# A four-layer graph network: the order of instructions planned with small GpSimd operations as users of the port shared with VectorE

## Chip, cores, metric

One core of one Trainium2 chip runs the whole kernel. The metric is device time in microseconds of one execution; the kernel before took 2909.99 us (median of 3 runs, 2907.28 to 2910.49).

## What is computed

32 graphs (batches) of 512 nodes with 128 features each, and a 0/1 adjacency matrix per graph with some 16 neighbours per node. Four layers, each on relu(layernorm(x)) and added to x:

```python
# layer 0: max over neighbours of relu(p_i + q_j + b)
p = h @ (W1 - W2); q = h @ W2
x = x + max_j(relu(p[:, :, None] + q[:, None, :] + b) * adj[..., None])
# layer 1: four steps, earlier features concatenated in the last two
src_agg = l2norm(adj, 2) @ (f @ ws + bs); dst_agg = l2norm(adj, 1).T @ (f @ wd + bd)
f = tanh(concat(src_agg, f @ wn + bn, dst_agg) @ wu + bu)
# layer 2: row-normalised aggregation
x = x + (adj / rowsum) @ (h @ weight) + bias
# layer 3: four GRU steps
m = adj.T @ (h @ weight[i]); h = gru_cell(m, h)
```

## The kernel before, in words

**Work.** Function `batch` makes the instructions of one graph: `prepare` (normalisation, transposed adjacency `at`, the table of q rows in DRAM, neighbour counts `cc` and `ccd`, keys of the remaining neighbours), `gathers` (layer 0), `layer1` and `layer23`. Features are held as 128 x (4 x 128) tiles, one PSUM bank each. Aggregations (`pg`) run as pairs of fp32r matmuls, one with `hi`, the value rounded to fp32r, and one with `lo`, the rest: ACT writes `hi`, VectorE (for `xn` GpSimd) writes `lo = source - hi`, and the matmuls follow (`parts`, L956, and `sbuf_parts`).

Layer 0's maximum comes from two sources. For each of four blocks of 128 columns and each of four slots, a one-hot matrix `oh` (VectorE compares `ccd` with a number, 128 x 1024) picks rows of q by matmul (`pa`), and VectorE takes the maximum into `acc`: 32 of these a batch. What is left, up to seven neighbours a node, comes by indirect DMA from the table on GpSimd's queue into `G`, 28 a batch, and VectorE takes the maximum into `gm` (L1127), 24 a batch.

A normalisation (`norm`) is done four times a batch: statistics on VectorE, then on GpSimd `rstd` as a power (a tensor_tensor on 128 x 4, L924) and `shift` as a product (128 x 4, L927), then `xn` on ACT. Before layer 1, GpSimd also works out the degrees' scales on 128 x 8 and 128 x 4 tiles (`dm`, `vectors`, `g`, `dinv`). In each GRU step, VectorE makes `nn`, ACT the tanh, GpSimd `zc = 1 - z` and the wide product `gate = h * z` (128 x 512, L1331), VectorE `nn * zc` and `h`; then `ph` transposes, and `hi` and `lo` follow for the next step.

**Order.** No order is written out by hand. Class `Flow` collects the operations, each with a planned cost, and works out when each engine issues what, in the manner of a list scheduler; the program's instruction order on each engine is the order in which `step` (L481) takes them. On the chip, the engines follow these queues and wait for each other's semaphores.

- `start` (L466) tells when an operation could begin: inputs ready, engine free, buffer free, and, for one with `port` set, not before `self.port`, the planned end of the last operation that uses the port (L477, L512). So no two marked operations overlap in the plan.
- Of those that can begin first, `step` takes the one with the earliest due time. `close` (L436) sets it: the place of the batch times `PACE`, less the length of the work behind it, less a lead. `LEADS` holds the lead of each stage, `LEADS0` and `LEADSN` what is added for the first and the last batch.
- `FIRST` and `LAST` shift the places of the first and last batches (L1365), and `WEIGHTS` gives the places of the three parts that load and fold the weights (`first`, `rest`, `last`). Up to six parts are open at once (`AHEAD`), so batches interleave. `SPACING` keeps the maxima of the gathered rows apart. `FIRST`'s fourth and `LAST`'s fifth value: the former is used from batch 3 on, the latter is not used with 32 batches.
- Buffers come in rings and are given out in the order in which the parts asked for them: `w3` of part `last` uses the buffer `nn` (L816), after the four `bfull` of part `rest` (L801).
- Where the plan has a gap of over 1 us on TensorE, it fills in matmuls without use (`spin`).

Every operation is noted by `Engine.note`, which marks the port's users (L295 to L298): on VectorE and on GpSimd's operations whose names begin with `tensor`, those with two inputs in SBUF of 64 or more elements per partition, and VectorE's tensor_scalar in any case. Issued instructions carry line L529 in the profile, where the plan calls them; they are told apart by their tiles.

## Time and profile before

| | |
|---|---|
| median of 3 runs | 2909.99 us |
| profiled execution, its own time | 2910.69 us |
| its span in the profile | 2909.0 us |
| granted TensorE clock, mean | 0.993 |
| busy: PE, DVE, ACT, POOL | 2795.8, 2299.1, 1268.4, 1848.5 us |
| wide GpSimd products `gate`, 128 x 512 | 124, mean 1365 ns |
| GpSimd `rstd` power, 128 x 4 | 128, mean 1193 ns |
| GpSimd `shift` product, 128 x 4 | 128, mean 287 ns |
| VectorE `gm` maximum, 128 x 128 | 768, mean 322 ns |
| VectorE `oh` compare, 128 x 1024 | 492, mean 723 ns |

PE stands for TensorE's matmuls, PEld for its weight loads, DVE for VectorE, ACT for ScalarE, POOL for GpSimd. A line of a group or a timeline names the tile that is written, then those that are read. A wait `A <- B: total, times, longest` is idle time of A's engine that B ended. The span of 2909.0 us leaves 1.7 us of the execution's time around it.

### The profile page before, as it was taken

To read this page: it belongs to the slowest core of one execution; us is meant where nothing else is said; L and a number is where in the kernel's file an instruction comes from. 1 tells how busy PE (TensorE), PEld (TensorE's weight loads), DVE (VectorE), ACT (ScalarE), POOL (GpSimd) and SP (SyncE) were. 2 spreads that over 40 slices of the span, in tenths; PEclk is the share of its full clock that TensorE was granted. 3 is DMA by queue.
4 is the path that set the end of the run, shared out by engine and by line. 5 is a ranking of instruction groups with operands and counts; after the bars stand their busy time and mean duration, and the time that the engine had idled before them with its cause. 6 is when DMAs were issued, how large, how long until landed. Compare 5 with 4: busy or idle time off the path is not lost.

```text
span 2909.0 us, 38588 instructions
## 1 busy us (share of the span) xinstructions
PE 2795.8 (96%) x11766; PEld 1794.6 (62%) x11766; DVE 2299.1 (79%) x5371; ACT 1268.4 (44%) x2622; POOL 1848.5 (64%) x2020
## 2 busy tenths in 40 slices
PE   7799999999999999999999999999999999999998
PEld 4565566666666665666665666666666666566675
DVE  6778888788888888888788888888888888887634
ACT  6643344444444443444443444444444444443333
POOL 3666656666666766666766666776666666666522
PEclk9999999999999999999999999999999999999999
DMA  6644334323444433334423344433344433333200
GB/s 150 136 74 88 62 85 81 83 55 76 79 86 81 83 60 78 74 83 80 87 56 78 74 84 87 82 69 64 74 84 87 81 81 56 70 66 63 55 5 9
DMA packets 191270, 218.49 MB, mean 75 GB/s; under 512 B 30376, under 2 KB 139600, under 8 KB 191056
## 3 DMA queue, kind: packets, MB, share of 16 engines
q0 software_dynamic: 47104, 92.34, 23.1%
q1 hardware_dynamic: 73768, 63.63, 7.1%
q10 hardware_dynamic: 70184, 59.98, 6.8%
q8 instruction: 96, 1.57, 0.2%
q14 instruction: 118, 0.97, 0.1%
HBM read 164.32 MB, written 17.96 MB: 63 GB/s over the span
## 4 chain that ended last, share of the span: by engine, by line
PE 85%; DVE 7%; DMA 2%; issue 2%; ACT 2%; POOL 1%; SPq 0%; ACTq 0%; DVEq 0%; POOLq 0%
PE pg L529 26%; PE pu L529 19%; PE pk L529 14%; PE pa L529 7%; PE phn L529 4%; PE pxn L529 4%; DVE acc L529 3%; PE ph L529 2%; PE pq L529 2%; PE pkey L529 2%; PE pt L529 1%; DVE lo L529 1%; PE pf L529 1%; PE po L529 1%; PE px L529 1%
## 5 line engine op out<-in xcount | busy, mean ns | idle before, releaser
L529 POOL DMA_INDIRECT G<-qtab,idx x768 | 841.3, 1095 | 653.6 <-DVE gm L529 495.3
L529 DVE TENSOR_TENSOR acc<-acc,pa 128x512 f32<-128x512 f32 x992 | 673.4, 679 | 123.3 <-PE pa L529 97.6
L529 PE MATMUL pg<-an,lo 128*128 128x512 f32 (+1 forms) x1072 | 461.9, 433 | 0.0
L529 PE MATMUL pg<-an,hi 128*128 128x512 f32 (+1 forms) x1072 | 456.1, 428 | 4.8 <-PE spin L553 1.1
L529 PE MATMUL pa<-oh,qhl 128*128 128x512 f32 x1024 | 450.5, 508 | 6.1 <-DVE acc L529 2.1
L529 PE MATMUL pu<-ag,w 128*128 128x512 f32 (+1 forms) x952 | 448.0, 568 | 4.1 <-DVE ag L529 4.1
L529 DVE TENSOR_SCALAR oh<-ccd 128x1024 fp32r<-128x1024 bf16 x492 | 348.9, 723 | 62.4 <-PE pa L529 55.0
L529 ACT ACTIVATE xn<-x,shift,rstd 128x128 f32<-128x128 f32 x512 | 214.6, 483 | 261.4 <-POOL shift L529 255.7
L529 PE MATMUL pg<-at,lo 128*128 128x512 f32 (+1 forms) x672 | 295.9, 442 | 22.8 <-DVE lo L529 22.3
L529 PE MATMUL pg<-at,hi 128*128 128x512 f32 (+1 forms) x672 | 272.7, 407 | 8.4 <-ACT hi L529 7.2
L529 PEld LDWEIGHTS pa<-oh,qhl 128*128 128x128 f32 x1024 | 191.8, 193 | 135.5 <-issue 65.9
L529 PEld LDWEIGHTS pg<-an,hi 128*128 128x128 f32 x1072 | 202.6, 189 | 107.2 <-issue 62.5
L529 PEld LDWEIGHTS pg<-an,lo 128*128 128x128 f32 x1072 | 202.7, 189 | 85.9 <-issue 52.0
L529 PE MATMUL pk<-h,g_hh 128*128 128x512 f32 (+1 forms) x528 | 246.7, 582 | 1.2 <-DVE ag L529 1.1
L529 DVE TENSOR_TENSOR gm<-gm,G 128x128 f32<-128x128 f32 x768 | 242.4, 322 | 3.5 <-DMA G<-qtab,idx 3.3
L529 PE MATMUL pk<-mT,g_ih 128*128 128x512 f32 (+1 forms) x528 | 243.3, 580 | 0.5 <-ACT mT L529 0.5
L529 PEld LDWEIGHTS pu<-ag,w 128*128 128x128 f32 x952 | 177.0, 189 | 107.7 <-issue 80.3
L529 ACT ACTIVATE gate<-pk,bsum 128x512 f32<-128x512 f32 (+1 forms) x264 | 176.7, 672 | 151.3 <-PE pk L529 148.7
L529 DVE TENSOR_TENSOR ag<-pg,rbc 128x512 f32<-128x512 f32 (+1 forms) x272 | 172.5, 653 | 71.5 <-PE pg L529 69.7
L529 DVE SCALAR_TENSOR_TENSOR nn<-phn,bcol,gate 128x512 f32<-128x512 f32 (+1 forms) x132 | 96.3, 729 | 148.2 <-ACT gate L529 148.1
L529 ACT COPY mT<-pg 128x512 f32<-128x512 f32 (+1 forms) x164 | 94.3, 575 | 272.9 <-PE pg L529 265.4
L529 POOL TENSOR_TENSOR rstd<-rstd,mhalf 128x4 f32<-128x4 f32 x128 | 152.7, 1193 | 86.9 <-DVE shift L529 82.6
(178 smaller groups left out, 5146.7 us busy)
## 6 DMA issues: line engine op xcount, KB each, us to landing
af<-in_adj_dram ACTq DMA_DIRECT2D x32, 1024.0 KB
ccd<-cc SPq DMA_DIRECT2D x512, 64.0 KB
an<-in_adj_dram POOLq DMA_DIRECT2D x128, 256.0 KB, 3.4
x<-in_x_dram ACTq DMA_DIRECT2D x64, 256.0 KB
rbc<-scal SPq DMA_DIRECT2D x32, 512.0 KB
G<-qtab,idx POOLq DMA_INDIRECT x768, 3.9
qtab<-qn SPq DMA_DIRECT2D x128, 64.0 KB
out_dram<-xo ACTq DMA_DIRECT2D x32, 256.0 KB
```

The source lines that it names most:

```text
L529: op.fn(*(real(v) for v in op.args), **{k: real(v) for k, v in op.kw.items()})
```

## The change

The mark of the port's users is widened: on GpSimd, an operation whose name begins with `tensor` and that has more than one input in SBUF is now marked, whatever its size. That adds the power and the product of each normalisation, and of the scales the power, `g`, `dinv` and the difference into `vectors`; those with one tensor input (`dm`, `has`, the copies) stay unmarked. The planner's numbers are replaced: `PACE`, `SPACING`, all leads but one, `FIRST`, `LAST`, `WEIGHTS`. What is computed, the tiles, the buffers and the planner's costs stay.

```diff
--- before.py
+++ after.py
@@ -33,39 +33,39 @@
 CODES = ((0, 1), (P, 1), (2 * P, 2), (4 * P, 4))
 ONACT = (2, 2, 1, 0)
 NLEFT = 7
-PACE = 46.14
-SPACING = 1.5
+PACE = 46.21
+SPACING = 1.6
 AHEAD = 6
 BANKS = (1, 2, 2, 1)
 
 LEADS = {
-    "prepare": -28.3, "counts": -7.5, "keys": 16.5, "rows": 26.6,
-    "gather0": 59.4, "gather1": 70.0, "gather2": 28.0, "gather3": 53.5,
-    "first": 61.2, "layer1": 43.0, "layer10": 30.3, "layer11": 8.7,
-    "layer12": 56.0, "layer13": -41.3, "layer2": 39.7, "layer3": 5.5,
-    "layer30": 99.5, "layer31": 189.8, "layer32": 213.5, "layer33": 84.7,
-    "out": 56.0,
+    "prepare": -28.3, "counts": 31.4, "keys": 20.4, "rows": 36.3,
+    "gather0": 70.0, "gather1": 75.0, "gather2": 44.1, "gather3": 65.1,
+    "first": 71.0, "layer1": 67.5, "layer10": 34.6, "layer11": 10.8,
+    "layer12": 54.1, "layer13": -65.5, "layer2": 38.2, "layer3": -10.5,
+    "layer30": 194.3, "layer31": 203.4, "layer32": 212.8, "layer33": 61.6,
+    "out": 87.1,
 }
 
 LEADS0 = {
-    "prepare": 18.5, "counts": 53.1, "keys": 4.8, "rows": -15.7,
-    "gather0": 52.2, "gather1": 93.4, "gather2": -34.5, "gather3": -69.1,
-    "first": 0.5, "layer1": 141.7, "layer10": 10.1, "layer11": 110.3,
-    "layer12": -73.8, "layer13": -13.4, "layer2": 6.9, "layer3": 56.5,
-    "layer30": 35.3, "layer31": 29.8, "layer32": 117.9, "layer33": 64.0,
-    "out": 75.9,
+    "prepare": 16.8, "counts": 45.5, "keys": -53.7, "rows": 3.2,
+    "gather0": 48.0, "gather1": 111.6, "gather2": 10.0, "gather3": 31.0,
+    "first": 77.1, "layer1": 209.2, "layer10": 0.7, "layer11": 111.5,
+    "layer12": -121.4, "layer13": -40.0, "layer2": -47.4, "layer3": 77.7,
+    "layer30": -5.6, "layer31": 99.0, "layer32": 161.7, "layer33": 176.6,
+    "out": 115.8,
 }
 LEADSN = {
-    "prepare": -19.9, "counts": -18.3, "keys": -42.0, "rows": 46.6,
-    "gather0": 15.9, "gather1": -47.7, "gather2": -77.8, "gather3": -4.3,
-    "first": 13.3, "layer1": -33.7, "layer10": 14.0, "layer11": -36.5,
-    "layer12": 103.7, "layer13": 62.6, "layer2": 212.2, "layer3": 99.8,
-    "layer30": 182.6, "layer31": 105.8, "layer32": 85.0, "layer33": 161.6,
-    "out": -15.2,
+    "prepare": 54.1, "counts": 28.9, "keys": -55.6, "rows": 8.4,
+    "gather0": 36.6, "gather1": -111.0, "gather2": -41.4, "gather3": -58.4,
+    "first": 0.8, "layer1": 3.9, "layer10": 6.0, "layer11": 6.3,
+    "layer12": 124.9, "layer13": 106.3, "layer2": 260.5, "layer3": 98.5,
+    "layer30": 146.5, "layer31": -13.0, "layer32": 15.9, "layer33": 155.6,
+    "out": -150.5,
 }
-FIRST = (1.57, 0.36, -0.05, 0.0)
-LAST = (0.0, 0.18, 0.33, 0.24, 0.3)
-WEIGHTS = (-3.98, -2.44, -5.94)
+FIRST = (1.4, 0.75, 0.18, 0.0)
+LAST = (0.0, -0.73, -1.07, -1.18, -4.34)
+WEIGHTS = (-4.28, -2.74, -9.33)
 
 LATE = {
     "xn2": ("xn0", 1), "hi2": ("qn", 1), "lo2": ("gm", 1), "mT": ("acc", 1), "hg": ("hT0", 1),
@@ -295,7 +295,8 @@
             tensors = [v for v in ins if v.free_size() >= 64 and in_sbuf(v)]
             fast = self.name == "vec" and op == "tensor_scalar"
             if self.name == "vec" or (self.name == "pool" and op.startswith("tensor")):
-                self.flow.part[-1].port = fast or len(tensors) > 1
+                two = self.name == "pool" and sum(in_sbuf(v) for v in ins) > 1
+                self.flow.part[-1].port = fast or two or len(tensors) > 1
 
         return note
 
```

## The prediction

> **What bounds the kernel now.** I read five views in this order: busy times on the page, windows of one batch length, TensorE's waits, the timelines around its idle stretches, and what VectorE's port users cost beside each kind of GpSimd work.

> The page, engines first:

> ```profile
> PE 2795.8 (96%) x11766; PEld 1794.6 (62%) x11766; DVE 2299.1 (79%) x5371; ACT 1268.4 (44%) x2622; POOL 1848.5 (64%) x2020
> PE   7799999999999999999999999999999999999998
> ```

> TensorE is busy all along but for the start and the end. Windows of 86.4 us (columns: stretch, its length, then busy us and count of PE, PEld, DVE, ACT, POOL, granted clock, DMA share, GB/s) show a loop that repeats exactly:

> ```profile
> 20.00:106.40 86.40, 60.06 (x334) 39.61 (x335) 61.09 (x149) 62.18 (x136) 44.28 (x58) 0.90 0.71 148
> 106.40:192.80 86.40, 75.58 (x420) 57.76 (x419) 70.17 (x189) 49.56 (x99) 61.53 (x67) 0.96 0.51 100
> ...
> 797.60:884.00 86.40, 84.77 (x352) 53.97 (x352) 71.47 (x167) 37.70 (x78) 57.86 (x63) 1.00 0.39 77
> 884.00:970.40 86.40, 84.77 (x352) 53.95 (x352) 71.42 (x167) 37.69 (x78) 58.07 (x63) 1.00 0.38 77
> ```

> One batch takes 86.4 us, TensorE is busy 84.77 of it and VectorE 71.4. Matmul ends are modelled, so I also summed starts: where they are dense, the start of the next comes 228 ns after a 128x512 fp32r matmul, 429 after a pass of an fp32 one, 109 after a 128x128 transpose. By these, a batch has 82.0 us of matmul work, 0.65 us of filling matmuls (spin) and 3.7 us of idle time. So an order can win at most 4.4 us a batch, and it can lose any amount. The waits say at what:

> ```profile
> PE pg L529 <- DVE lo L529: 22.3, 25, 1.1
> PE spin L553 <- DVE lo L529: 9.4, 25, 0.7
> ```

> 25 times each: two places in each batch of the loop. Here is the first, in the timelines of TensorE, VectorE and GpSimd (start, us, engine, work):

> ```profile
> 987.43 0.50 PE L529 MATMUL pg<-at,hi 128*128 128x512 f32 x1 [0.23 <-ACT hi L529]
> 987.91 0.51 PE L529 MATMUL pg<-an,hi 128*128 128x512 f32 x1
> 989.31 0.50 PE L529 MATMUL pg<-at,lo 128*128 128x512 f32 x1 [0.89 <-DVE lo L529]
> ```
> ```profile
> 985.95 1.31 DVE L529 TENSOR_TENSOR gm<-gm,G 128x128 f32<-128x128 f32 x1
> 987.18 1.47 DVE L529 TENSOR_TENSOR acc<-acc,pa 128x512 f32<-128x512 f32 x2
> 988.57 0.68 DVE L529 TENSOR_TENSOR lo<-pf,hi 128x512 fp32r<-128x512 f32 x1
> ```
> ```profile
> 985.80 1.31 POOL L529 TENSOR_TENSOR gate<-h,gate 128x512 f32<-128x512 f32 x1
> ```

> The gm maximum takes 1.31 us instead of its median of 0.28, because GpSimd's wide product began just before it. That pushes two acc maxima and then lo by 1.03 us, and the aggregation waits for lo. This place costs 1.9 us a batch by matmul starts. The second (ph, then hi, then lo, then the aggregation with an) costs 1.5 us, spin included, and has no such collision in it.

> [...] I sorted the trace's port users of VectorE by what they overlap most: gm beside a wide GpSimd instruction takes 1175 ns (34 of them), beside an rstd power 281 (36), beside nothing 280. oh takes 997, 692 (30) and 683. One such pair:

> ```profile
> 528.48 0.69 DVE L529 TENSOR_SCALAR oh<-ccd 128x1024 fp32r<-128x1024 bf16 x1 [0.69 <-PE pa L529]
> ```
> ```profile
> 528.04 1.17 POOL L529 TENSOR_TENSOR rstd<-rstd,mhalf 128x4 f32<-128x4 f32 x1
> ```

> The oh lies inside the power's 1.17 us and loses nothing. [...]

> **The change, part by part.** (1) *The mark.* It adds 12 GpSimd instructions a batch to the planner's port users: 4 rstd powers (mean 1193 ns), 4 shift products (287), the power and the difference into vectors (1681, 219), g (216) and dinv (208): 4.77 + 1.15 + 1.68 + 0.22 + 0.22 + 0.21 = 8.25 us. The wide ones were marked already. Nothing is added to the program: no instruction, wait or DMA; only the order on each queue changes. If the mark kept every small one clear of VectorE, VectorE would win 0.4 us in the whole run (all of its lengthening of over 60 ns beside small ones), and GpSimd some 19 us (128 x (1193 - 1044, the fastest tenth)) + 12 us (128 x (287 - 193)), about 1 us a batch on an engine at 64%. Behind GpSimd's shift stands ACT's xn, for which TensorE waits 8.6 us in all, nearly all before the loop. Value taken: 0; bounds 0 to -8.

> (2) *What the false exclusion does to the order.* VectorE's port users are about 55 a batch (24 gm, 15 oh, 4 nn products, 4 h, junk, qhl and small scalars). In the plan each now meets a small GpSimd instruction with a chance of 8.25 / 86.4 = 9.5%, and is put back by about half of 1.1 us: 55 x 0.095 x 0.5 = 2.6 us a batch of delay that the chip doesn't have. The planner answers by putting something else first. Where oh or gm moves, acc work hides it (TensorE waits 2.1 us for oh in the whole run). Where nn or h is put behind an acc or oh (0.7 us each), the next GRU step starts later, and what is late is hi, then lo: the waits above. I take a fifth (nn and h are 8 of 55, with something for lo being displaced): 0.5 us x 25 = +13. Bounds: 0, as the planner may fill with other batches' work, to +28 (one full 1.1 us displacement a batch at one of the two places). A gain is not excluded either: any new order draws the collisions anew, rival one below.

> (3) *Leads, pace, spacing.* PACE moves by 0.15%, nothing. SPACING 1.5 to 1.6 stretches the 24 spaced gathers from 36 to 38.4 us of 86.4: room enough, 0. The leads permute who goes first among ready work; they cost nothing by themselves.

> (4) *The start.* The last weights get a place of -9.33 instead of -5.94, 156 us earlier, and the middle ones 14 us earlier, while batch 0 goes 8 us later. Before, TensorE waits for two of these loads:

> ```profile
> PE pg_hh L529 <- DMA graw_hh<-in_L_gnn_w_hh_dram: 4.6, 1, 4.6
> PE pw3t L529 <- DMA w<-in_L_gnn_weight_dram: 4.0, 1, 4.0
> ```

> w3 can't be loaded before bfull of the middle weights gives up its buffer (73.8 us; the load starts at 74.1), so only a part moves: half of 8.6, -4. Each of these loads is queued on SP or ACT ahead of batch 0's transfers, so the other bound is +8; at the end, with the last batches' leads redrawn, 0, with +-8.

> Sum on the profiled execution (2910.7, span 2909.0): 0 + 13 + 0 - 4 = +9, so 2920; the median of the runs, 2910.0, is 0.7 lower and gives the same to within rounding.

> **The rivals.** *Faster: the collision leaves the path.* The order is drawn anew, and if the gate product no longer starts just ahead of gm and lo, lo comes 1.03 us earlier; the copy hi ends at 987.37, so it doesn't hold lo back. 25 x 1.03 = -26, and -4 at the start: 2880. For it: the place is one accident of the loop, repeated 25 times, and the plan already forbids the overlap, so it is a slip of the chip against the plan. Against it: the mark doesn't touch wide products, and GpSimd has five kinds of them, 13 us a batch, so another can collide on the path at the same price. It decides from 0.25 us a batch on. *No difference: the small marks dodge nothing that matters.* The loop's two places stay, start and end cancel: 2910. For it: GpSimd's small instructions are off TensorE's path. Against it: some 70 changed numbers hardly leave the same order. *The change does what it says, small collisions being real:* worth 0.4 us on VectorE, so it also gives 2910 and counts with that case. *A second collision on the path:* slower by up to 25 x 1.55 (lo's 1.16 and hi's 0.39) = 39, so 2949; it is the upper part of my forecast's case.

> **Chances.** Slower, my forecast with its upper part, 0.49 (own range 2916 to 2955); faster 0.36 (2868 to 2904); no difference 0.15. A measurement here can tell about 0.2% (6 us) from no change. The sign hangs on one 1 us stall, which is why the two sides lie close; slower leads because the added constraint is one that the trace denies. The range takes from 2878, near the faster rival, to 2952, the second collision: about 2 in 10 lie outside.

> **What would show it.** Right: a loop of about 86.9 us with the same 82.0 us of work; oh, gm and h beside rstd as short as before; waits of pg for lo longer or more; the pw3t and pg_hh waits smaller. Wrong: a loop of 85.4 us or less with gm near lo at 0.28 us; or oh beside rstd getting shorter than 0.68; or most of the difference in the first 200 us, which I put at 4.

## The result, and the profile after

After: 2926.1 us, median of 5 runs (2924.78 to 2940.35), beside 2907.28 us for before (5 runs, 2906.57 to 2910.49). The ratio is 1.0073, 95% interval 1.0058 to 1.0088: slower by 19 us. The profiled execution is the longest of the five (2940.35 us, span 2938.6; granted clock 0.986). A second profile of the same kernel, `after_again` below, has a span of 2924.6 us, nearer to the median; the account below has both, and the text goes by this one.

The page after, busy time by engine:

```profile
PE 2803.4 (95%) x11694; PEld 1789.2 (61%) x11694; DVE 2390.3 (81%) x5371; ACT 1251.0 (43%) x2622; POOL 1837.9 (63%) x2020
```

Same work, 72 fewer filling matmuls, and VectorE is busy 91 us longer with the same 5371 instructions. That is the first hint: something makes VectorE's instructions longer (36 of the 91 us are nn*zc, 24 h, 15 oh). Windows of one batch length:

```profile
797.60:884.00 86.40, 84.35 (x349) 53.21 (x348) 75.26 (x167) 37.01 (x78) 57.82 (x63) 1.00 0.40 77
884.00:970.40 86.40, 84.34 (x343) 53.17 (x342) 73.68 (x165) 36.19 (x77) 56.41 (x62) 0.98 0.40 77
```

VectorE rose from 71.4 to 75.3 us in the first of them. The loop no longer repeats exactly: the second window has a granted clock of 0.98 and fewer instructions on each engine, so it holds less than a batch. TensorE's waits:

```profile
PE ph L530 <- DVE h L530: 37.2, 54, 1.1
PE pu L530 <- DVE ag L530: 15.6, 6, 3.0
PE pg L530 <- DVE acc L530: 10.1, 25, 3.1
PE pa L530 <- DVE acc L530: 9.6, 28, 0.7
```

The waits of pg and spin for VectorE's lo (22.3 and 9.4 us) are gone from the top; in their place TensorE's transposes `ph` wait for `h`, the output of a GRU step (4.6 us before), and `pu` for `ag`. Here is the last GRU step of one batch, first before, then after:

```profile
1075.56 0.68 DVE L529 TENSOR_TENSOR nn<-nn,zc 128x512 f32<-128x512 f32 x1
1076.16 0.68 DVE L529 TENSOR_TENSOR acc<-acc,pa 128x512 f32<-128x512 f32 x1
1076.76 0.68 DVE L529 TENSOR_TENSOR h<-gate,nn 128x512 f32<-128x512 f32 x1
...
1077.88 0.60 PE L529 MATMUL ph<-ident,h 128*128 128x128 f32 x4
```

```profile
721.78 1.38 DVE L530 TENSOR_SCALAR oh<-ccd 128x1024 fp32r<-128x1024 bf16 x1
...
722.53 1.78 POOL L530 TENSOR_TENSOR gate<-h,gate 128x512 f32<-128x512 f32 x1
...
723.09 1.77 DVE L530 TENSOR_TENSOR nn<-nn,zc 128x512 f32<-128x512 f32 x1
...
724.79 1.47 DVE L530 TENSOR_TENSOR acc<-acc,pa 128x512 f32<-128x512 f32 x2
725.51 0.50 PE L530 MATMUL pa<-oh,qhl 128*128 128x512 f32 x1 [0.35 <-DVE acc L530]
726.17 0.28 DVE L530 TENSOR_TENSOR gm<-gm,G 128x128 f32<-128x128 f32 x1
726.37 0.68 DVE L530 TENSOR_TENSOR h<-gate,nn 128x512 f32<-128x512 f32 x1
...
727.11 0.66 PE L530 MATMUL ph<-ident,h 128*128 128x128 f32 x4 [1.09 <-DVE h L530]
```

The same wide product as before now meets `oh` and nn*zc (1.38 and 1.77 us in place of some 0.68). Two acc maxima, gm and h stand behind them on VectorE, so both `pa` and `ph` come late. Not all of oh's 1.38 us is the product's: GpSimd also issues a load of `an` beside it, and in `after_gate_narrow` below, where the product starts only behind oh, oh takes 0.99.

**The account.** From matmul starts, over the 24 batches between the fifth and the 29th store of the output, in us. "Half clock" is what matmuls lose in stretches with a granted clock of 0.5 (128x512 fp32r matmuls start 427 ns apart there, some 230 elsewhere); the wait columns leave these out. The columns don't add up to the loop: the two terms named in the text below, and waits and gaps too small for a column, are left out (some 34 us of them before, 40 in after_again).

| | loop | work | spin | ph for h | pg for lo of pf | pg or spin for lo of ph | pa, pg for acc | pu for ag | half clock |
|---|---|---|---|---|---|---|---|---|---|
| before | 2077.3 | 1968.8 | 13.6 | 1.4 | 25.4 | 11.1 | 5.5 | 0.6 | 1.6 |
| after, first profile | 2107.8 | 1968.1 | 0.6 | 40.2 | 0 | 1.0 | 22.7 | 16.6 | 18.5 |
| after_again | 2095.9 | 1968.1 | 0.6 | 40.0 | 0 | 1.0 | 22.7 | 8.3 | 15.3 |

Outside the loop little changed: span less loop is 831.7 us before and 830.8 after (828.7 in after_again). In the loop, before to after_again: the lo of pf gave 25.4, ACT's hi ahead of it 8.7, and the spin place 29.6 (13.6 + 11.1 + 6.5 behind the filling matmuls, less 1.6). That is 63.7 us gained. Lost: h 38.6, acc 17.2, the clock 13.7, ag 7.7, and some 6 in small pieces (work is 0.7 less). The net is +18.6; the medians differ by 18.8 (the two profiles by 15.6, as after_again is 3 us shorter outside the loop).

So a gain twice as large as rival one's came, and more was lost.

### The profile page after: what moved, and what is told of

It reads as the page before. It is cut to its first block, busy times and chain, and to the rows that moved or that the text cites. A ratio compares the mean times of both kernels' runs of the same rounds, so it can differ in the third digit from the quotient of the medians.

```text
span 2938.6 us, 37886 instructions
## 1 busy us (share of the span) xinstructions
PE 2803.4 (95%) x11694; PEld 1789.2 (61%) x11694; DVE 2390.3 (81%) x5371; ACT 1251.0 (43%) x2622; POOL 1837.9 (63%) x2020
## 4 chain that ended last, share of the span: by engine, by line
PE 75%; DVE 13%; issue 4%; DMA 3%; ACT 2%; POOL 2%; SPq 0%; DVEq 0%; ACTq 0%; POOLq 0%
PE pg L530 22%; PE pu L530 17%; PE pk L530 13%; PE pa L530 5%; DVE acc L530 4%; PE phn L530 3%; PE pxn L530 3%; DVE nn L530 3%; PE ph L530 2%; DVE h L530 2%; DMA ccd<-cc 2%; PE pkey L530 2%; PE pq L530 1%; DVE oh L530 1%; PE pt L530 1%
## 5 line engine op out<-in xcount | busy, mean ns | idle before, releaser
L530 POOL DMA_INDIRECT G<-qtab,idx x768 | 799.2, 1041 | 787.7 <-DVE gm L530 610.8
L530 PE MATMUL pa<-oh,qhl 128*128 128x512 f32 x1024 | 506.0, 540 | 15.4 <-DVE acc L530 9.6
L530 PE MATMUL pu<-ag,w 128*128 128x512 f32 (+1 forms) x952 | 455.4, 571 | 15.6 <-DVE ag L530 15.6
L530 PE MATMUL pg<-an,hi 128*128 128x512 f32 (+1 forms) x1072 | 444.4, 416 | 8.1 <-DVE acc L530 7.0
L530 DVE TENSOR_SCALAR oh<-ccd 128x1024 fp32r<-128x1024 bf16 x492 | 367.7, 755 | 60.9 <-PE pa L530 38.1
L530 PE MATMUL pg<-at,lo 128*128 128x512 f32 (+1 forms) x672 | 312.0, 466 | 2.0 <-POOL lo L530 1.7
L530 PE MATMUL pg<-at,hi 128*128 128x512 f32 (+1 forms) x672 | 287.3, 430 | 4.5 <-DVE acc L530 3.1
L530 ACT CAST hi<-ph 128x512 fp32r<-128x512 f32 (+1 forms) x99 | 56.7, 572 | 406.5 <-PE ph L530 401.6
L530 POOL TENSOR_TENSOR rstd<-rstd,mhalf 128x4 f32<-128x4 f32 x128 | 152.9, 1195 | 59.6 <-DVE shift L530 57.0
L530 POOL TENSOR_TENSOR gate<-h,gate 128x512 f32<-128x512 f32 (+1 forms) x132 | 184.7, 1400 | 6.8
```

Of the source, the lines that this page charges most:

```text
L530: op.fn(*(real(v) for v in op.args), **{k: real(v) for k, v in op.kw.items()})
```

## The experiments

Theory after the result: the wide product's collision with `oh` and nn*zc makes h late (27 us or more of the 40), and TensorE's idle time there halves its clock, which costs the rest. Rival: the mark's false exclusions, or the new numbers, spread delay over the whole order, and the collision is only where it shows.

### The mark and the numbers, apart

`mark_only` is before with the new definition of `port`; `numbers_only` is after with the old one; `pace_only` is before with PACE 46.21; `spacing_only`, run later, is before with SPACING 1.6. `after_again` is after, unchanged.

```diff
 # mark_only: before with
+                two = self.name == "pool" and sum(in_sbuf(v) for v in ins) > 1
-                self.flow.part[-1].port = fast or len(tensors) > 1
+                self.flow.part[-1].port = fast or two or len(tensors) > 1
 # pace_only: before with                 # spacing_only: before with
-PACE = 46.14                             -SPACING = 1.5
+PACE = 46.21                             +SPACING = 1.6
```

> The kernel before with the mark on GpSimd's small two-operand instructions alone, all numbers as before. If the false exclusion costs time by itself (my step 2): slower than 2907 by 10 to 50 us. If only the new numbers cost time: 2907 within 6 us. Any new order also draws stalls and halvings anew, which could give 2890 to 2960.

> The changed kernel's numbers with the mark as it was before. If the new numbers are at fault: 2926 us or more. If the mark is at fault: under 2910. If the numbers fit only the mark that they were found with: slower than 2926.

> The changed kernel itself, for a second profile: the first one was of an execution of 2940 us, the others took 2925 to 2927. Clock theory: the same order and the same stalls, but fewer halvings in the loop (7 to 8 by the mean clock of 0.988, 14 in the first profile), [...]; 24 batches in some 2093 us where the first profile has 2108. Rival (the 14 us are something else, such as late transfers): as many halvings, and the 14 us in waits for transfers.

> The kernel before with PACE 46.21 instead of 46.14 and nothing else, as a control for the run with the mark alone. If any other order unfits the numbers: slower by 30 us or more, the length of a batch irregular (80 to 110 us) as with the mark alone. If the mark itself cost the 104 us: 2907 within 10 us, batches of 86.4 us.

> The kernel before with one number of the planner changed, SPACING 1.6 in place of 1.5: neither the mark nor the leads. The order that comes out differs from that of before nearly everywhere, about as widely as in the run with the mark alone (3012.6). If any order planned with numbers that were not fitted to it loses about as much, this run gives 2970 to 3080, and the 104 us of the mark alone say nothing on the mark. If the mark itself is what hurt there, this run stays under 2940.

| | median, us | runs | ratio to before, 95% interval |
|---|---|---|---|
| mark_only | 3012.61 | 4 | 1.0358, 1.0342 to 1.0375 |
| numbers_only | 3066.05 | 4 | 1.0533, 1.0517 to 1.055 |
| after_again | 2928.27 | 4 | 1.0078, 1.0063 to 1.0094 |
| pace_only | 2909.02 | 12 | 1.0012, 1.0003 to 1.002 |
| spacing_only | 3030.5 | 4 | 1.0415, 1.0399 to 1.0431 |

The mark alone costs 104 us, the numbers alone 158, both together 19: the two are not terms of a sum. `spacing_only` says why. One number, with no mark, costs 121, and nearly every matmul of TensorE then stands elsewhere in its order. In all three the loop never settles: a batch takes 80 to 108 us, while before it takes 86.4 in most cases and never less than 85.4 or more than 88.2. The losses lie everywhere (in spacing_only, gaps are 174 us of the loop; the largest single one, ph for h, is 15.5). So a loss of this size says that the planner's numbers don't fit, and nothing of the mark. Whether the mark by itself helps or hurts, with numbers fitted to it, these runs can't tell. `pace_only` is a weak control: only about one matmul in twenty stands elsewhere.

### The collision alone: a quarter of the product

`after_gate_narrow` is after, with the product h*z of the last GRU step made on 128 of its 512 columns. The order is that of after.

```diff
+                if l == W.NL3 - 1 and step == NT:
+                    F.part[-1].fn = lambda *v: nc.gpsimd.tensor_mul(*(x[:, 0:1, :] for x in v))
```

> The changed kernel, same order, but GpSimd's product h*z of the last GRU step of batches 0 to 30 takes 128 of 512 columns (three quarters of that product are left out). Collision theory: nn*zc falls from 1.77 to about 0.7 us, h and TensorE's transposes come 1.0 us earlier, a batch of the loop takes 85.2 us instead of 86.24, [...] 2885 to 2900 us. Rival (the acc maxima queued ahead of h, not the collision, hold it): 2920 to 2926 us. Rival (the time sits in the clock alone): as the first by halvings, but a batch stays at 86.2 us, 2910 to 2920 us.

2875.54 us (2869.34 to 2880.15), ratio 0.9888 (0.987 to 0.9907): 51 us less than after, more than either theory had. The same place in its timeline:

```profile
1140.64 0.99 DVE L530 TENSOR_SCALAR oh<-ccd 128x1024 fp32r<-128x1024 bf16 x1
...
1141.55 0.67 DVE L530 TENSOR_TENSOR nn<-nn,zc 128x512 f32<-128x512 f32 x1
1141.78 0.76 POOL L1334 TENSOR_TENSOR gate<-h,gate 128x128 f32<-128x128 f32 x1
...
1144.47 0.66 PE L530 MATMUL ph<-ident,h 128*128 128x128 f32 x4 [0.23 <-DVE h L530]
```

nn*zc is back to 0.67 us, and ph waits 0.23 us in place of 1.09. In the loop, ph for h falls from 40.0 to 12.6, the wait of pa for acc (10.3) is gone, half clock falls from 15.3 to 1.3. The loop is 45 us shorter than that of after_again: the expectation's sum had neither pa nor the clock in it.

What is left of ph for h is mostly another collision. Of the 12.6 us, 9.7 lie at another GRU step (9.6 in after_again as well), where h itself meets another wide GpSimd instruction, the addition of layer 2's bias into `x`:

```profile
788.42 1.27 POOL L530 TENSOR_TENSOR x<-x,b 128x512 f32<-128x512 f32 x1 [0.28 <-ACT xn L530]
788.56 1.68 DVE L530 TENSOR_TENSOR h<-gate,nn 128x512 f32<-128x512 f32 x1
...
790.38 0.63 PE L530 MATMUL ph<-ident,h 128*128 128x128 f32 x4 [0.30 <-DVE h L530]
```

At the last step, where after_again waits 28.4 us, 1.7 are left, with the two acc maxima and gm ahead of h as before.

### The collision moved: the whole product, earlier

`after_gate_early` computes everything. Only GpSimd's own order changes: each gate product goes out directly behind `zc = 1 - z`, which reads the same z (the expectation below calls it the z product).

```diff
-        op.fn(*(real(v) for v in op.args), **{k: real(v) for k, v in op.kw.items()})
+        if not op.sent:
+            op.fn(*(real(v) for v in op.args), **{k: real(v) for k, v in op.kw.items()})
...
+        pair = op.pair
+        if pair and not pair.waits:
+            pair.fn(*(real(v) for v in pair.args), **{k: real(v) for k, v in pair.kw.items()})
+            pair.sent = True
...
+                zcs.append(F.part[-1])
...
+                zcs[c.start // step].pair = F.part[-1]
```

> The kernel after; only GpSimd's own order differs: each 128x512 gate product h*z is issued directly behind the z product that it reads, in place of later in the stream. In the trace of after, z stands at about 1153.9 us of a batch and the gate product would run from there to about 1155.2, ahead of VectorE's nn*zc (1156.3), which it now hits. If the collision of the wide product with nn*zc is what makes the last step's h late (the run with a quarter of the product gave 2875.5), the computation being whole here: nn*zc back to about .68 us, TensorE's waits of ph for h under 15 us in all (40 before), the acc waits of pa and pg under 5, at most 4 halvings of the clock in the loop, 2870 to 2895 us. The rival, that the gain of the quarter-width run came from less work on GpSimd and not from the place of the collision, or that the product moved early collides with VectorE's oh or rstd beside it: 2910 to 2930 with the waits moved to another name.

2891.92 us (2887.68 to 2897.3), ratio 0.9947 (0.9934 to 0.9961): 34 us less than after, by nothing but the place of one kind of instruction on one queue, and faster than before.

```profile
1142.32 1.30 POOL L543 TENSOR_TENSOR gate<-h,gate 128x512 f32<-128x512 f32 x1
1142.85 0.68 DVE L532 TENSOR_TENSOR acc<-acc,pa 128x512 f32<-128x512 f32 x1
1143.45 0.72 DVE L532 TENSOR_SCALAR oh<-ccd 128x1024 fp32r<-128x1024 bf16 x1
...
1144.09 0.68 DVE L532 TENSOR_TENSOR nn<-nn,zc 128x512 f32<-128x512 f32 x1
...
1147.02 0.66 PE L532 MATMUL ph<-ident,h 128*128 128x128 f32 x4 [0.44 <-DVE h L532]
```

The product now runs beside acc (one of its inputs lies in PSUM), which takes 0.68 us here, as it does in after beside such a product (median of 61) and beside nothing; the product is over when nn*zc begins. ph for h is 12.05 us in the loop, pa and pg for acc 11.9, half clock 1.6; pg now waits 6.5 us for a lo, which it did not in after_again. Of the 12.05 us, 10.6 lie at this last step, with nn*zc short. At the other step h now starts just ahead of the addition into `x`, and it is the addition that takes longer:

```profile
1130.67 0.68 DVE L532 TENSOR_TENSOR h<-gate,nn 128x512 f32<-128x512 f32 x1
1130.74 1.74 POOL L532 TENSOR_TENSOR x<-x,b 128x512 f32<-128x512 f32 x1 [0.29 <-ACT xn L532]
```

The waits for acc stay above the expected 5 us, and the expectation's "nn*zc back to 0.68" holds for the last step alone: in two of the other steps nn*zc still takes 1.76 us beside its own product, off TensorE's path. The rival, less work on GpSimd, is out: all of the product is there.

### The clock alone: filling matmuls in after

`after_fill` is after in the same order, with four filling matmuls ahead of the last step's transposes.

```diff
+                if 2 <= int(name.split("_")[1]) < 30:
+                    for _ in range(4):
+                        self.nc.tensor.matmul(
+                            flat(tile.real), self.fill[0], self.fill[1], start=True, stop=True
+                        )
```

> The changed kernel, same order on every engine, plus four filling matmuls (0.86 us) ahead of the transposes of the last GRU step of batches 2 to 29, where TensorE stands idle for 1.4 us. Clock theory (the loop loses its time because 3.4 us windows with TensorE under some 42% busy are followed by 3.4 us at half clock, and by a late ccd transfer in consequence): halvings in the loop fall from 14 to at most 3, time 2895 to 2908 us. Rival (the loop is slower through its plain idle time, whatever the clock): 2926 us, unchanged. Rival (transfers are late by themselves): the 3 us waits for ag every fourth batch stay, 2915 to 2926 us.

2928.58 us (2927.73 to 2930.4), ratio 1.0068 (1.0054 to 1.0081): as after, a miss. The halvings in the loop are gone but for two of ten (half clock 15.3 to 2.7), and the loop is only 2.4 us shorter (2093.5). The kernel issues four filling matmuls a batch and the trace has three, with a double gap between two of them in 20 of the 24 batches: records are missing. At 216 ns each, the 96 take 20.7 us. They wait 11.25 for acc, whose maximum last read their PSUM bank; what is left of the wait for h is 12.3, 10.0 of it at the other step. Together 44, where the wait for h and the little filling of after_again make 40.6. So of the 12.6 us that the clock gave back, 2.4 came out as time, some 4 went into the filling, and some 6 into small waits (xn, top, ag, gaps too short to assign). So that a halved clock follows from the idle time is shown: same order, less idle, two halvings for ten. The 42% of the expectation fits the first profile of after, where half clock followed windows that were active for 0.41 or less (last section); that a late ccd transfer comes of it isn't shown. That half clock costs its 15 us is not shown either: here little of it came out as time, though the filling took time of its own, so how much of it is a loss by itself stays open.

What a halving looks like, in the windows of after (PE busy by modelled ends, granted clock, DMA share, GB/s):

```profile
724.98:728.39 3.41, 1.96 (x9) 1.00 0.00 1
728.39:731.81 3.42, 3.42 (x9) 0.51 0.42 96
731.81:735.20 3.39, 3.39 (x19) 0.99 0.52 114
```

The stretch with the late h (the timeline above) is followed by one at half clock, with 9 matmuls in it where the next has 19.

### Before, without its filling matmuls, and with its own collision removed

`before_nofill` leaves out the loop's filling matmuls; the order of the rest stays. `nofill_gate_early` is that with the edit of `after_gate_early`; `before_gate_early` is before with that edit alone. `nofill_gate_late`, tried first, issued the gate product behind the following load of `an` instead.

```diff
-                for args in work:
+                for args in work if not 300.0 < t < 2500.0 else []:
```

```diff
 # nofill_gate_late: in step
+        if op.gate:
+            self.held = op
+        else:
+            op.fn(*(real(v) for v in op.args), **{k: real(v) for k, v in op.kw.items()})
+            if op.engine == "pool" and self.held:
+                self.release()
```

> The kernel before, same order, without the 81 filling matmuls that its plan puts into the loop (three a batch, 0.65 us). Clock theory: [...] at least 8 halvings in the loop where there were 2, 2920 to 2955 us. Rival (filling matmuls have no use here, plain idle time counts): 2907 us, or some us less.

> The kernel before without the loop's filling matmuls, and with the wide product h*z issued after the load of an that follows it on GpSimd's queue (26 times; nothing else moves). Collision theory: gm takes 0.28 us again instead of 1.31, lo comes 1.0 us earlier, a batch takes 84.5 us instead of 85.52, 2888 falls to 2858 to 2868 us. Rival (hi, an acc or another collision is as late): 2880 to 2888 us. Rival (h now comes later and stalls TensorE in its turn): 2888 or more.

> The kernel before without the loop's filling matmuls (2887.8), and with the gate products issued directly behind their z products on GpSimd's queue. The collision of gm with the wide gate product, which the forecast's rival put at about 1 us a batch of waiting of pg for lo, should go: gm back from 1.31 to about .5 us or less. If that wait is on the path: lo<-pf waits of 25 us in the loop drop below 10, batch base 85.5 to about 84.8, 2865 to 2880 us. If another wait stands right behind it (pg for an or acc), or the product collides elsewhere: 2885 to 2900.

> The kernel before with one edit: on GpSimd's queue each wide gate product stands directly behind the z product that it reads; the filling matmuls stay. This is the forecast's faster rival done alone (gm no longer meets the gate product: 2880 there, of which 26 us from the loop and 4 from the start). Without the filling matmuls the same edit gave 23.7 us. If the two places of a batch are independent: 2883 to 2889, waits of pg for lo down from 22.3 to under 10, those of spin for lo at 9.4 as before. If the filling matmuls take part of it (their plan times no longer fit, or the wait of spin for lo grows): 2893 to 2908.

| | median, us | runs | ratio to before, 95% interval | loop | pg for lo of pf | for lo of ph | half clock |
|---|---|---|---|---|---|---|---|
| before_nofill | 2887.8 | 5 | 0.9929, 0.9915 to 0.9942 | 2058.1 | 25.5 | 11.15 | 0 |
| nofill_gate_late | 2912.07 | 19 | 1.0018, 1.0011 to 1.0025 | 2083.1 | 25.5 | 11.15 | 13.0 |
| before_gate_early | 2878.63 | 4 | 0.9901, 0.9884 to 0.9917 | 2056.1 | 11.9 | 11.1 | 0 |
| nofill_gate_early | 2864.07 | 5 | 0.9844, 0.983 to 0.9857 | 2039.0 | 12.0 | 11.15 | 0 |

`before_nofill` was a miss, by sign: the clock stays whole without the filling. The second place of a batch in before and in before_nofill:

```profile
1030.87 0.69 DVE L529 TENSOR_TENSOR lo<-ph,hi 128x512 fp32r<-128x512 f32 x1 [0.25 <-ACT hi L529]
...
1031.61 0.81 PE L553 MATMUL spin<-code,identb 128*128 128x512 bf16 x3 [0.36 <-DVE lo L529]
...
1032.57 0.47 PE L529 MATMUL pg<-an,hi 128*128 128x512 f32 x1
```

```profile
1021.79 0.69 DVE L529 TENSOR_TENSOR lo<-ph,hi 128x512 fp32r<-128x512 f32 x1 [0.24 <-ACT hi L529]
1022.53 0.50 PE L529 MATMUL pg<-an,hi 128*128 128x512 f32 x1 [0.36 <-DVE lo L529]
```

The filling matmuls wait for the same lo as the aggregation that they should bridge to, 0.36 us, because lo is the last reader of the bank that they write. They start when the wait is over, and the aggregation comes 0.96 us after them; a batch takes 86.4 us with them and 85.5 without.

`nofill_gate_late` was a miss too, and a useful one. With the product behind the load, gm's record starts first, and gm still ends with the product:

```profile
980.19 1.84 DVE L539 TENSOR_TENSOR gm<-gm,G 128x128 f32<-128x128 f32 x1
980.59 1.28 POOL L555 TENSOR_TENSOR gate<-h,gate 128x512 f32<-128x512 f32 x1
```

The product takes its usual 1.28 us, and gm 1.84 in place of 0.28. At 0.28 us gm would have been over before the product's start; what held it until then isn't shown (GpSimd issued the load of `an` at that time). The loop is 25 us longer than that of before_nofill: 13.0 are half clock, and pg now waits for acc (13.8 us by TensorE's waits, 1.6 in before_nofill). Keeping the product clear of gm is what helps. In nofill_gate_early the product runs 1 us ahead of gm, at the place that the forecast showed:

```profile
970.47 1.30 POOL L542 TENSOR_TENSOR gate<-h,gate 128x512 f32<-128x512 f32 x1
970.83 0.69 DVE L531 TENSOR_TENSOR acc<-acc,pa 128x512 f32<-128x512 f32 x1 [0.39 <-PE pa L531]
...
971.44 0.47 DVE L531 TENSOR_TENSOR gm<-gm,G 128x128 f32<-128x128 f32 x1
...
973.22 0.68 DVE L531 TENSOR_TENSOR lo<-pf,hi 128x512 fp32r<-128x512 f32 x1
...
973.96 0.51 PE L531 MATMUL pg<-at,lo 128*128 128x512 f32 x1 [0.31 <-DVE lo L531]
```

gm takes 0.47 us in place of 1.31, the wait of pg for lo 0.31 in place of 0.89. The same edit with the filling kept (before_gate_early) ends below its expectation: 28 us, 21 of them in the loop, most of the rest ahead of it (first output stored at 273.4 us, before at 280.4). Of the 21, the wait of pg for lo gives 13.5; it halves and does not vanish. Without the filling it gives 24. At 2864.07 us nofill_gate_early is 1.56% faster than before, and the fastest of all.

## Why the prediction was right, and where it was not

The time lies inside the range, slower as forecast, 6 us above the predicted one. The reasons did less well than the number. The change is twice the forecast one (19 us for 9), and it is what is left of two larger sums, some 64 us won and 82 lost, of which the forecast's sum had nothing of the gain and 13 of the loss: that the sign came out is in part luck.

- **What bounds the kernel.** Right. Work stayed at 82.0 us a batch (1968.8 and 1968.1 us in 24), and all that moved is idle time, filling and clock. "An order can lose any amount" is what spacing_only and its like show.
- **(1) The mark, 0.** Right that small collisions cost VectorE nothing. After, gm beside an rstd power has a median of 280 ns (53 of them), beside nothing 283; oh 690 (55) and 685. GpSimd's rstd is not shorter for the mark: 1195 ns, before 1193. So on VectorE the mark had nothing to win.
- **(2) The false exclusion, +13.** The step that failed. Its picture, "nn or h is put behind an acc or oh", is in the trace: h of the last step stands behind two acc maxima and a gm, where before it stood behind one acc. But with the collision on nn*zc gone, and the same instructions ahead of h, the wait at that place falls from 28.4 us to 1.7 in after_gate_narrow and to 10.6 in after_gate_early: what the place in the order costs lies between these, and that the mark put h there isn't shown. Most of the loss has another cause: the wide product hits nn*zc, 27 us of ph for h and 10 of pa for acc, and the addition into x hits h of another step, some 10 more. That is the mechanism of rival four, "a second collision on the path", which I had priced at up to 39 and folded into this step as its upper end. I also named the wrong victim: late was h, while the waits for lo that I let grow vanished.
- **(3) Pace, spacing, leads, 0.** Right for PACE. Wrong for the others taken singly: SPACING alone costs 121 us, all numbers without the mark 158. "Room enough" looked at the time that gathers have, not at the order, in which one such number moves nearly everything.
- **(4) Start and end, -4.** The wait for w3's weights went, as said, but that for graw_hh is 8.2 us in one profile and 2.8 in the other, and the first output is stored at 281.3 and 278.2 us, before at 280.4. No gain that can be told from the spread.
- **Rival one, 2880.** Its price was right as a sum: with the gate products moved in before, and gm's collision gone with that, before_gate_early is at 2878.6. Its parts were not: the wait of pg for lo fell by 13.5 us and not by 26; earlier outputs and the waits for acc gave the rest. In after that collision did leave the path, and with it the spin place, 63.7 us in all; the new collisions, the clock, ag and small pieces took some 82 back.
- **Not foreseen.** The halving of the clock, 13.7 us by the account; how much of it is a loss by itself is open. The late transfers: in three batches of after_again (five in the first profile) VectorE's oh waits 2.6 to 4.2 us for a transfer, of ccd in all but one, and pu for ag behind it, most of the 8.3 us; this stays in every version of after, with or without halvings. A 1 MB load of af is issued near that ccd, but 0.1 us ahead of its last part in only two of these eight batches, and 0.7 behind it in the others, as in batches without such a wait: the cause is open. And I counted spin as harmless, where it cost 20 us.

## What to carry to other kernels

Before a planner is given a finer rule, look in the trace at what the existing rule misses: here wide products still met VectorE on the path (gm 1.31 us in place of 0.28 before, nn*zc 1.77 in place of 0.68 after), although the plan lets no two of them overlap, and one rule (send the product out as soon as its input is there; acc beside it kept its 0.68 us) was worth 28 us in before, where the new mark had nothing to win. A stall that an order removes is worth its price only if the new order brings none of the same kind, so price both sides. Judge one part of a fitted set of numbers only with the set fitted anew, and check that filling matmuls don't wait for the very thing that they should bridge.
